# Softmax attention of a fused transformer block: score tiles of one PSUM bank in a written TensorE order, and sign projections as two products in fp32r

## The chip, the cores and the metric

The kernel runs on one core of one Trainium2 chip. The metric is the device time of one execution in microseconds. The kernel before takes 1735.04 us, the median of three runs (1726.19 to 1746.35). All profile numbers of the kernel before come from one profiled execution that took 1739.77 us.

## The reference, cut to what matters

Two batches of 1024 tokens with 512 features go through half a feed-forward layer, an attention layer and half a feed-forward layer again. The attention layer has 32 query heads of 16 features and 8 key and value heads, each of which serves four query heads. Its four projections use only the signs of their weights, with one scale for each output.

```python
def bitnet_linear(x, weight, scale_param):
    s = jnp.maximum(jnp.mean(jnp.abs(weight), axis=1), 1e-08)
    binary_w = jnp.sign(weight / s[:, None])
    y = jnp.einsum('bsi,oi->bso', x, binary_w)
    y = y * (s * scale_param)[None, None, :]
    return jnp.nan_to_num(y, nan=0.0, posinf=1000000.0, neginf=-1000000.0)
...
scores = jnp.einsum('bhqd,bhkd->bhqk', q, k) / np.sqrt(HEAD_DIM)
attn = jax.nn.softmax(scores, axis=-1)
out = jnp.einsum('bhqk,bhkd->bhqd', attn, v)
...
x = x + 0.5 * ffn(layernorm(x)); x = x + attention(layernorm(x)); x = x + 0.5 * ffn(layernorm(x))
```

Softmax is taken over all 1024 keys, without a mask, and the largest score of each query is subtracted ahead of the exponential.

## The kernel before, in words

Everything is in 32-bit floats. [...]operands of type F32R are multiplied in one pass with fewer mantissa bits, so a value that must be kept to full precision is split into a high part and the rest, and both are multiplied.

For each batch the kernel runs these stages: `ffn` (L152) on two groups of 512 tokens; `qkv` (L241) on the same groups; `attention` (L283); then for each group `o_proj` (L392), `ffn` and the store. For the first batch `binarize` (L218) turns the four projection weights, which the POOL queue loads at the start, into signs after the first `ffn`.

`qkv` makes the normalized input transposed (`ln_T`, L130), multiplies it with the sign weights in F32 (L255, L274), scales it on ScalarE (L258), replaces values that are not numbers (`nan_to_num`, L115: three or four VectorE instructions and one on GpSimd), and splits it into the high part and the rest on GpSimd (L261, L262). For queries 16 small DMAs on SP's queue for each chunk of 128 features (L268) put the parts in `qn`: each head has 32 rows, 16 of the high part and 16 of the rest, and four heads that share a key head fill the 128 rows.

`attention` works on one key head (four query heads) at a time. `place` (L287) copies the key's two parts to the four row groups with 16 DMAs on SP's queue (L293). `maxima` (L297) multiplies queries by keys (L308) and takes the largest score of each query on VectorE, 1024 scores in an instruction (L311). After 512 queries the maxima are transposed (L318), split on VectorE (L320, L321) and put by 8 DMAs on SP's queue (L327) in the tile `mq`. `scores` (L330) multiplies keys by queries again, now with keys on the rows of the output (L340), adds the negative maxima as one more product with a matrix of ones (L344), and takes the exponential on ScalarE, 1024 scores in an instruction (L347). `values` (L353) multiplies the exponentials by the values and by a column of ones, so the sums come out beside the outputs (L357, in F32); after 1024 keys the result is transposed (L364) and divided by the sums (L367, L368).

The loop at L376 runs `scores` of one key head and `maxima` of the next one in 16 alternating steps; each step also has the `values` of the step before. A score tile `p` covers two PSUM banks, and a pool of three such tiles (`psb`) is shared by `maxima`, `scores` and parts of `ffn`. Other products use a pool of two single banks (`pss`). `kT` and `mq` have two buffers.

The order of instructions on each engine is made when the program is built: a scheduler takes, for each engine, the instruction that it reckons to be ready first, earlier ones of the program ahead of later ones, and a tile can't be taken before its buffer is free. On the chip each engine works through its own list in that order, and so does SP's queue of DMAs.

Of the kernel before, what the change touches and what calls it, by code (L numbers as in the profile page):

```python
# [32 lines left out]
def macaron_kernel(ctx: ExitStack, tc: tile.TileContext, x_in, wbT, b_base, wrT, aT, bT,  # L33
# [11 lines left out]
    p3 = ctx.enter_context(tc.tile_pool(name="p3", bufs=3))  # L45
    tmp = ctx.enter_context(tc.tile_pool(name="tmp", bufs=7))
    sm = ctx.enter_context(tc.tile_pool(name="sm", bufs=4))
    ps_b = ctx.enter_context(tc.tile_pool(name="ps_b", bufs=3, space=bass.MemoryType.PSUM))
    ps_s = ctx.enter_context(tc.tile_pool(name="ps_s", bufs=2, space=bass.MemoryType.PSUM))

    def t512(name):
        return tmp.tile([P, 512], F32, tag="t512", name=name)

    def psb(name):
        return ps_b.tile([P, 2, 512], F32, tag="psb", name=name)

    def pss(name):
        return ps_s.tile([P, 512], F32, tag="pss", name=name)
# [21 lines left out]

    wq = const.tile([P, KC, D], F32, name="wq")
    wk = const.tile([P, KC, P], F32, name="wk")
    wv = const.tile([P, KC, P], F32, name="wv")
    wo = const.tile([P, KC, D], F32, name="wo")
    for t, src in ((wq, wqT), (wk, wkT), (wv, wvT), (wo, woT)):
        nc.gpsimd.dma_start(t, src.rearrange("(c p) n -> p c n", p=P))
# [20 lines left out]

    ones_r = const.tile([P, P], F32R, name="ones_r")
    nc.gpsimd.memset(ones_r.bitcast(F32), 1.0)
    vaug = big1.tile([P, NT, G, 32], F32, tag="vaug", name="vaug")  # L110
    nc.gpsimd.memset(vaug, 0.0)
    nc.gpsimd.memset(vaug[:, :, :, HD:HD + 1], 1.0)


    def nan_to_num(y, o, shape, n):  # L115
# [8 lines left out]
        nc.vector.tensor_scalar(lo_, y, 0.0, None, ALU.min)  # L124
# [5 lines left out]
    def ln_T(xt, n):  # L130
# [10 lines left out]
        xT = p2.tile([P, KC, GT], F32, tag="xT", name=f"xT{n}")  # L141
        for t in range(TG):
            xn = t512(f"xn{n}_{t}")
            nc.vector.tensor_scalar(xn, xt[:, t, :], mv[:, t, 0:1], rstd[:, t:t + 1],  # L144
                                    ALU.subtract, ALU.mult)
            pt = pss(f"pt{n}_{t}").rearrange("p (c q) -> p c q", c=KC)
            for c in range(KC):
                nc.tensor.transpose(pt[:, c, :], xn[:, c * P:(c + 1) * P], ident)  # L148
            nc.scalar.copy(xT[:, :, t * P:(t + 1) * P], pt)  # L149
        return xT  # L150

    def ffn(xt, n):  # L152

        xT = ln_T(xt, n)
        ph = psb(f"ph{n}").rearrange("p a (b n) -> p (a b) n", b=2)
        for t in range(TG):
            for c in range(KC):
                nc.tensor.matmul(ph[:, t, 0:ER + E], xT[:, c, t * P:(t + 1) * P], arw[:, c, :],  # L158
                                 start=(c == 0), stop=(c == KC - 1))
        lg = ph[:, :, ER:ER + E]  # L160
# [33 lines left out]
        for t in range(TG):  # L194
            nc.vector.tensor_tensor(
                hw[:, t * ER:(t + 1) * ER].rearrange("p (e r) -> p e r", e=E),
                ph[:, t, 0:ER].rearrange("p (e r) -> p e r", e=E),
                w01[0][:, t, :].unsqueeze(2).to_broadcast([P, E, R]), ALU.mult)
        pt = pss(f"hwp{n}")
# [4 lines left out]
        for t2 in range(TG // 2):  # L204
            pb = psb(f"pb{n}_{t2}")
            for j in range(2):
                t = 2 * t2 + j
                xb = t512(f"xb{n}_{t}")
                nc.gpsimd.tensor_tensor(xb, xt[:, t, :], bh, ALU.add)
                for c in range(KC):  # L210
                    nc.tensor.matmul(pb[:, j, :], xT[:, c, t * P:(t + 1) * P], wb[:, c, :],  # L211
                                     start=(c == 0), stop=False)
                nc.tensor.matmul(pb[:, j, :], hT[:, t * P:(t + 1) * P], lb, start=False, stop=True)  # L213
                nc.vector.scalar_tensor_tensor(xt[:, t, :], pb[:, j, :], 0.5, xb,  # L214
                                               ALU.mult, ALU.add)


    def binarize(w, n_out, name):  # L218
        ab = p2.tile([P, KC, GT], F32, tag="xT", name=f"ab_{name}")
        nc.scalar.activation(ab[:, :, 0:n_out], w, AF.Abs)  # L220
        pm = pss(f"pm_{name}")
        for c in range(KC):
            nc.tensor.matmul(pm[:, 0:n_out], ones, ab[:, c, 0:n_out],
                             start=(c == 0), stop=(c == KC - 1))
        s = tmp.tile([P, 512], F32, tag="t512", name=f"s_{name}")[:, 0:n_out]
# [5 lines left out]
        nc.scalar.activation(w, w, AF.Sign)  # L231
        return s

    def to_column(s, c, sc):

        pt = pss(f"col_{sc.name}_{c}")
# [4 lines left out]
    def qkv(b):  # L241

        qn = big1.tile([P, G, S], F32R, tag="qn", name=f"qn{b}")
        kn = [big1.tile([P, S], F32R, tag=f"kn{j}", name=f"kn{j}_{b}") for j in range(2)]
        for g in range(NG):
            n = f"a{b}_{g}"
            xT = ln_T(xg[b, g], n)
            cols = slice(g * GT, (g + 1) * GT)
            for c in range(KC + 1):
                w_, sc_ = (wq[:, :, c * P:(c + 1) * P], qsc[:, c:c + 1]) if c < KC else (wk, ksc)  # L250
                dst = ([p2.tile([P, 512], F32R, tag=f"qh{j}", name=f"qh{j}{n}_{c}") for j in range(2)]
                       if c < KC else [t[:, cols] for t in kn])
                pq = pss(f"pq{n}_{c}")
                for k in range(KC):
                    nc.tensor.matmul(pq, w_[:, k, :], xT[:, k, :],  # L255
                                     start=(k == 0), stop=(k == KC - 1))
                y = t512(f"y{n}_{c}")
                nc.scalar.activation(y, pq, AF.Copy, scale=sc_)  # L258
                z = t512(f"z{n}_{c}")
                nan_to_num(y[:, :], z[:, :], [P, 512], f"{n}_{c}")  # L260
                nc.gpsimd.tensor_copy(dst[0], z)  # L261
                nc.gpsimd.tensor_tensor(dst[1], z, dst[0].bitcast(F32), ALU.subtract)  # L262
                if c < KC:

                    for h in range(2 * REP):
                        for j in range(2):
                            r = 32 * (h % REP) + HD * j
                            nc.sync.dma_start(  # L268
                                qn[r:r + HD, 2 * c + h // REP, cols].bitcast(F32),
                                dst[j][h * HD:(h + 1) * HD, :].bitcast(F32))  # L270
            pv = pss(f"pv{n}").rearrange("p (t v) -> p t v", t=TG)
            for t in range(TG):
                for k in range(KC):
                    nc.tensor.matmul(pv[:, t, :], xT[:, k, t * P:(t + 1) * P], wv[:, k, :],  # L274
                                     start=(k == 0), stop=(k == KC - 1))
            y = t512(f"yv{n}").rearrange("p (t v) -> p t v", t=TG)
# [196 lines left out]
```

## Time and profile before

| | |
|---|---|
| time of the profiled execution | 1739.77 us |
| its span | 1738.0 us |
| median of three runs | 1735.04 us |
| busy: TensorE, VectorE, ScalarE, GpSimd | 1370.9, 950.0, 583.5, 147.5 us |
| TensorE clock granted, mean | 0.877 |
| 0 to 98 us | `ffn` of the first batch, `binarize` |
| 98 to 207.8 us; 950 to 1060 us | `qkv` and the first `place`, batch 0 and 1 |
| 207.8 to 789 us; 1060 to 1624 us | `attention`, batch 0 and 1 |
| 789 to 899 us; 1624 to 1738 us | `o_proj`, `ffn`, store, batch 0 and 1 |
| 899 to 950 us | `ffn` of batch 1 |

A row of the profile's groups names line, engine, operation, output and inputs, shapes and count; then come the busy time, the mean duration of one in ns, and the idle time of the engine ahead of it with what ended it. PE is TensorE, PEld its weight loads, DVE VectorE, ACT ScalarE, POOL GpSimd and SPq the queue of SP. In a timeline a row has the start, the length in us, the instruction and how many were merged, and in brackets the idle time ahead.

### The profile page before, as it was taken

What the parts mean: (1) busy time and instruction counts of PE and PEld (TensorE: products, weight loads), DVE (VectorE), ACT (ScalarE), POOL (GpSimd) and SP (SyncE); (2) the same over time, 40 slices, a digit from 0 to 9 for tenths busy, and PEclk for the clock granted to TensorE, in tenths of its full rate; (3) what the DMA queues carried; (4) which work ended last, traced back from release to release, by engine and by line L of the source; (5) the groups of instructions that cost most, each with busy time, mean ns of one, the idle gap of its engine ahead of it and who ended that gap; (6) DMA issues with size and microseconds to landing.
All of it is one profiled execution on the core that took longest, in us unless ns stands there. A gap on an engine that the chain in (4) does not pass through costs nothing.

```text
span 1738.0 us, 21741 instructions
## 1 busy us (share of the span) xinstructions
PE 1370.9 (79%) x8741; PEld 633.6 (36%) x8741; DVE 950.0 (55%) x1322; ACT 583.5 (34%) x653; POOL 147.5 (8%) x146
## 2 busy tenths in 40 slices
PE   5784398888888888897799806888888888888796
PEld 3442143333333333334354403433333333333353
DVE  3753276566665655624544616756665666663443
ACT  1210014354443434472011100344453444446310
POOL 3433000000000000002021420000000000000111
PEclk9897559799997979998999855799997989999898
DMA  4012400100101101000110223010110101100000
GB/s 159 0 27 47 72 2 1 25 16 11 25 2 25 21 6 26 1 2 0 49 49 1 45 49 53 2 26 1 25 17 11 26 1 26 22 5 2 1 25 24
DMA packets 31587, 40.31 MB, mean 23 GB/s; under 512 B 17264, under 2 KB 17776, under 8 KB 31488
## 3 DMA queue, kind: packets, MB, share of 16 engines
q1 hardware_dynamic: 28800, 34.13, 9.8%
q0 software_dynamic: 960, 3.21, 0.5%
q10 hardware_dynamic: 1728, 1.59, 0.3%
q8 instruction: 69, 1.13, 0.3%
q14 instruction: 30, 0.25, 0.0%
HBM read 9.00 MB, written 4.19 MB: 8 GB/s over the span
## 4 chain that ended last, share of the span: by engine, by line
PE 63%; ACT 13%; DVE 10%; SPq 7%; issue 3%; POOL 2%; DMA 2%; ACTq 0%; POOLq 0%; DVEq 0%
PE av L357 16%; PE p L308 14%; ACT es L347 12%; PE p L340 10%; SPq L268 6%; PE p L344 5%; DVE mn L311 3%; PE pbs L211 2%; PE pbf L211 2%; PE po L404 2%; PE pqa L255 2%; PE avT L364 1%; SPq L293 1%; PE mp L318 1%; PE phs L158 1%
## 5 line engine op out<-in xcount | busy, mean ns | idle before, releaser
L311 DVE TENSOR_REDUCE mn<-p 128x2 f32<-128x1024 f32 x512 | 617.9, 1221 | 402.1 <-PE p L308 399.1
L347 ACT ACTIVATE es<-p 128x1024 f32<-128x1024 f32 x512 | 499.2, 1022 | 730.1 <-PE p L344 714.4
L308 PE MATMUL p<-kT,qn 32*128 32x512 f32 x2048 | 400.4, 483 | 234.5 <-ACT es L347 125.6
L308 PEld LDWEIGHTS p<-kT,qn 32*128 32x128 f32 x2048 | 195.4, 213 | 404.0 <-ACT es L347 211.0
L357 PE MATMUL av<-es,vaug 128*32 128x512 f32 x2048 | 316.0, 656 | 0.1
L340 PE MATMUL p<-qn,kT 32*128 32x512 f32 x2048 | 269.8, 479 | 14.1 <-DVE mn L311 14.1
L340 PEld LDWEIGHTS p<-qn,kT 32*128 32x128 f32 x2048 | 115.3, 201 | 246.2 <-ACT es L347 140.0
L344 PE MATMUL p<-mq,ones_r 2*128 2x512 f32 x1024 | 163.8, 427 | 0.0
L127 POOL TENSOR_SCALAR ro<-yo 128x512 f32<-128x512 f32 x16 | 11.6, 723 | 1326.1 <-DVE yo L125 1303.7
L344 PEld LDWEIGHTS p<-mq,ones_r 2*128 2x128 f32 x1024 | 79.8, 203 | 20.6 <-issue 9.0
L357 PEld LDWEIGHTS av<-es,vaug 128*32 128x32 f32 x2048 | 43.4, 111 | 105.3 <-issue 100.4
L367 DVE RECIPROCAL rc<-avT 128x16 f32<-128x16 f32 x32 | 8.2, 258 | 125.1 <-PE avT L364 125.1
L255 PE MATMUL pqa<-xTa,wq 128*128 128x512 f32 x128 | 60.0, 629 | 2.8 <-ACT xTa L149 2.8
L211 PE MATMUL pbs<-wb,xTs 128*128 128x512 f32 x128 | 59.8, 597 | 0.9 <-DVE x L214 0.9
L211 PE MATMUL pbf<-wb,xTf 128*128 128x512 f32 x128 | 58.8, 594 | 0.0
L404 PE MATMUL po<-wo,aT 128*128 128x512 f32 x128 | 56.0, 595 | 0.5 <-ACT aT L400 0.5
L148 PE MATMUL pts<-ident,xns 128*128 128x128 f32 x64 | 14.8, 420 | 41.5 <-DVE xns L144 41.5
L149 ACT COPY xTs<-pts 128x512 f32<-128x512 f32 x16 | 9.3, 586 | 103.1 <-PE pts L148 103.1
L214 DVE SCALAR_TENSOR_TENSOR x<-pbs,xbs 128x512 f32<-128x512 f32 x16 | 11.1, 691 | 51.3 <-PE pbs L213 51.3
L320 DVE CAST mT<-mp 4x512 fp32r<-4x512 f32 x32 | 21.7, 679 | 31.4 <-PE mp L318 24.5
L364 PE MATMUL avT<-ident,avs 128*128 128x128 f32 x128 | 24.1, 297 | 18.3 <-ACT avs L361 17.4
L255 PEld LDWEIGHTS pqa<-xTa,wq 128*128 128x128 f32 x128 | 25.5, 202 | 35.3 <-issue 31.2
(172 smaller groups left out, 903.9 us busy)
## 6 DMA issues: line engine op xcount, KB each, us to landing
kT<-kn SPq DMA_DIRECT2D x256, 64.0 KB, 2.5
x<-in_x SPq DMA_DIRECT2D x4, 1024.0 KB, 6.2
qn<-qh0a SPq DMA_DIRECT2D x128, 32.0 KB, 2.0
qn<-qh1a SPq DMA_DIRECT2D x128, 32.0 KB, 1.9
mq<-mT SPq DMA_DIRECT2D x256, 2.0 KB, 1.7
out<-x SPq DMA_DIRECT2D x4, 1024.0 KB, 4.3
wb<-in_wbT ACTq DMA_DIRECT2D x1, 1024.0 KB, 20.4
wq<-in_wqT POOLq DMA_DIRECT2D x1, 1024.0 KB, 10.5
```

The costliest lines, as they stand in the source:

```text
L211: nc.tensor.matmul(pb[:, j, :], xT[:, c, t * P:(t + 1) * P], wb[:, c, :], start=(c == 0), stop=False)
L255: nc.tensor.matmul(pq, w_[:, k, :], xT[:, k, :], start=(k == 0), stop=(k == KC - 1))
L268: nc.sync.dma_start(qn[r:r + HD, 2 * c + h // REP, cols].bitcast(F32), dst[j][h * HD:(h + 1) * HD, :].bitcast(F32))
L308: nc.tensor.matmul(ps[:, j, :], qT[r0:r0 + 32, qt * P:(qt + 1) * P], kT[r0:r0 + 32, i, kh * 512:(kh + 1) * 512], start=(i == 1), stop=(i = ...
L311: nc.vector.tensor_reduce(mn[:, kh, qt % 4, 2 * hp:2 * hp + 2], ps, AX.X, ALU.max, negate=True)
L320: nc.vector.tensor_copy(mT[:, 0, :], pt[0:REP, :])
L340: nc.tensor.matmul(ps[:, j, :], kT[r0:r0 + 32, i, keys], qT[r0:r0 + 32, cols], start=(i == 1), stop=False)
L344: nc.tensor.matmul(ps[:, j, :], ones_r[r0:r0 + 2, :], mq[r0:r0 + 2, cols], start=False, stop=True)
L347: nc.scalar.activation(e, ps, AF.Exp, scale=HD ** -0.5)
L357: nc.tensor.matmul(av[0][32 * h:32 * h + 32, :], vaug[:, kt, g, :], es[h // 2][:, h % 2, :], start=(kt == 0), stop=(kt == NT - 1))
L364: nc.tensor.transpose(pt[:, t * P:(t + 1) * P], avs[:, t * P:(t + 1) * P], ident)
L404: nc.tensor.matmul(po, aT_[:, c, t * P:(t + 1) * P], wo[:, c, :], start=(c == 0), stop=(c == KC - 1))
```

## The change

Scores. A score tile is one bank of 512 columns for one head; seven banks form one pool `w` for all products, and one bank is kept for the outputs. A unit is now 512 queries of one key head, 16 in a batch, and takes four turns. A turn has eight tiles of maxima, `m`, in two passes each, eight tiles of exponentials, `e`, in three passes each (the third adds the maxima), and four parts `A` of the output product, each of 256 columns for four heads. The string `TURN` writes down the TensorE order of a turn; `manual_schedule` keeps TensorE to it, while the other engines are ordered by the scheduler as before. A unit's exponentials start five turns after its maxima, its outputs one turn later.

Queries and keys. `qkv` runs for one group and writes both parts of queries and keys to DRAM, two DMAs for each chunk. `place` reads them back with 8 DMAs for queries and 8 for keys for each unit, all on SP's queue; `q` and `k` have three buffers, `mq` two.

Sums. The output tile with its sums goes to DRAM in one DMA for each unit. `normalized` reads outputs and sums back (16 DMAs for each of four chunks in each group of queries), takes the reciprocals, writes them to DRAM (1 DMA) and reads them back spread over the rows (8 DMAs); GpSimd multiplies and splits, ScalarE makes the high part.

Projections. The sign weights are F32R, and inputs are a high part and the rest, so each F32 product becomes two F32R products (`qkv`, `o_proj`). `binarize` loads its weight when its turn comes. In `nan_to_num` the minimum goes from VectorE to GpSimd; the split's high part goes from GpSimd to ScalarE; in `o_proj` the last addition goes to GpSimd. In `ffn` the router's logits are copied out by ScalarE. All of `vaug` starts as ones.

```diff
-    tmp = ctx.enter_context(tc.tile_pool(name="tmp", bufs=7))
+    tmp = ctx.enter_context(tc.tile_pool(name="tmp", bufs=8))
-    ps_b = ctx.enter_context(tc.tile_pool(name="ps_b", bufs=3, space=bass.MemoryType.PSUM))
-    ps_s = ctx.enter_context(tc.tile_pool(name="ps_s", bufs=2, space=bass.MemoryType.PSUM))
+    ps = ctx.enter_context(tc.tile_pool(name="ps", bufs=7, space=bass.MemoryType.PSUM))
+    ps_a = ctx.enter_context(tc.tile_pool(name="ps_a", bufs=1, space=bass.MemoryType.PSUM))
...
-        nc.vector.tensor_scalar(lo_, y, 0.0, None, ALU.min)
+        nc.gpsimd.tensor_scalar(lo_, y, 0.0, None, ALU.min)
...
+            if halves:
+                nc.vector.tensor_tensor(xL[:, :, tok], pt, xT[:, :, tok].bitcast(F32), ALU.subtract)
...
+            nc.scalar.copy(lg[:, 2 * t2:2 * t2 + 2, :], ph[:, :, ER:ER + E])
...
+    def binarize(src, n_out, name):
+        w = p2.tile([P, KC, GT], F32, tag="xT", name=f"w_{name}")[:, :, 0:n_out]
+        nc.gpsimd.dma_start(w, src.rearrange("(c p) n -> p c n", p=P))
+        ab = p2.tile([P, KC, GT], F32, tag="xL", name=f"ab_{name}")[:, :, 0:n_out]
...
+        wr = const.tile([P, KC, n_out], F32R, name=f"sign_{name}")
+        nc.scalar.activation(wr, w, AF.Sign)
...
+    def qkv(b, g):
+        xs = ln_T(xg[b, g], n, True)
...
+            pq = bank(f"pq{n}_{c}")
+            for k in range(KC):
+                for j in range(2):
+                    nc.tensor.matmul(pq, w_[:, k, :], xs[j][:, k, :],
+                                     start=(k + j == 0), stop=(k + j == KC))
...
+            hi = t512(f"hi{n}_{c}", F32R)
+            nc.scalar.copy(hi, z)
+            lo = t512(f"lw{n}_{c}", F32R)
+            nc.gpsimd.tensor_tensor(lo, z, hi.bitcast(F32), ALU.subtract)
+            for j, t in enumerate((hi, lo)):
+                dst = qd[b][j, c * P:(c + 1) * P, cols] if c < KC else kd[b][j, :, cols]
+                nc.sync.dma_start(dst, t.bitcast(F32))
...
+    TURN = ("m0(0) e0(2) e0(7) e0(5) m1(0) e1(2) e1(5) e1(7) m0(4) e2(2) e2(7) m0(1) m1(4) m0(7) "
+            "m1(1) A0 A1 m1(7) e2(5) m0(6) e0(4) e0(3) e0(1) m1(6) e1(4) e1(3) e1(1) m0(2) e2(4) "
+            "e2(3) e2(1) m1(2) A2 m0(3) e0(0) e0(6) m0(5) m1(3) e1(0) e1(6) m1(5) e2(0) e2(6) A3")
+    TU = NT // 2
+    LEAD = TU + 1
...
+        def place(u):
...
+            q = p2.tile([P, 512], F32R, tag="q", name=f"q{n}", bufs=3)
+            for h in range(REP):
+                for j in range(2):
+                    r = 32 * h + HD * j
+                    f = (REP * g + h) * HD
+                    nc.sync.dma_start(q[r:r + HD, :].bitcast(F32), qd[b][j, f:f + HD, cols])
+            k = p2.tile([P, 2, S], F32R, tag="k", name=f"k{n}", bufs=3)
+            src = kd[b][:, g * HD:(g + 1) * HD, :].rearrange("i d s -> d i s")
+            for r in range(0, P, HD):
+                nc.sync.dma_start(k[r:r + HD, :, :].bitcast(F32), src)
...
+        def m_tile(u, i, p):
...
+            nc.tensor.matmul(s["m", i], s["q"][rows, qt * P:(qt + 1) * P],
+                             s["k"][rows, 1 - p, kh * 512:(kh + 1) * 512],
+                             start=(p == 0), stop=(p == 1))
+            if p == 1:
+                nc.vector.tensor_reduce(s["mn"][:, h, qt, kh:kh + 1], s.pop(("m", i)), AX.X,
+                                        ALU.max, negate=True)
...
+        def m_place(u):
+            pt = bank(f"mp{b}_{u}")
+            nc.tensor.transpose(pt[0:4 * REP, 0:P], s["mm"], ident)
+            mT = sm.tile([4 * REP, 2, P], F32R, tag="mT", name=f"mT{b}_{u}")
+            nc.vector.tensor_copy(mT[:, 0, :], pt[0:4 * REP, 0:P])
+            nc.vector.tensor_tensor(mT[:, 1, :], pt[0:4 * REP, 0:P], mT[:, 0, :].bitcast(F32),
+                                    ALU.subtract)
+            for h in range(REP):
+                for j in range(2):
+                    r = 32 * h + j
+                    nc.sync.dma_start(
+                        s["mq"][r:r + 1, :].bitcast(F32),
+                        mT[h * 4:(h + 1) * 4, j, :].bitcast(F32))
...
+        def e_tile(u, i, p):
...
+            if p < 2:
+                nc.tensor.matmul(t, s["k"][rows, 1 - p, kt * P:(kt + 1) * P], s["q"][rows, :],
+                                 start=(p == 0), stop=False)
+            else:
+                two = slice(32 * h, 32 * h + 2)
+                nc.tensor.matmul(t, ones_r[two, :], s["mq"][two, :], start=False, stop=True)
+                e = p2.tile([P, 512], F32, tag="es", name=f"es{b}_{u}_{i}", bufs=20)
+                nc.scalar.activation(e, s.pop(("e", i)), AF.Exp, scale=HD ** -0.5)
...
+        def a_part(u, kt, half):
...
+            if kt == NT - 1 and half == 1:
+                o = t512(f"avs{b}_{u}")
+                nc.scalar.copy(o, s["av"])
+                nc.sync.dma_start(ad[b][g, :, qb * 512:(qb + 1) * 512], o)
...
+        with tc.manual_schedule(engines={mybir.EngineType.PE}):
+            place(0)
+            for n in range(TU * len(units) + LEAD + 1):
+                m, e, a = todo(n, 0), todo(n, LEAD), todo(n, LEAD + 1)
+                if m and m[1] == 0 and m[0] + 1 < len(units):
+                    place(m[0] + 1)
+                for kind, p, i in turn:
...
+                        if p == 0 and n >= TU and (n % TU) == 0 and (n // TU - 1) < len(units):
+                            m_place(n // TU - 1)
...
+    def normalized(b, qb):
...
+        for c in range(KC):
+            rs = sm.tile([P, 32], F32, tag="rs", name=f"rs{n}")
+            z = t512(f"an{n}")
+            for g2 in range(2):
+                for h in range(REP):
+                    r = (g2 * REP + h) * HD
+                    nc.sync.dma_start(rs[r:r + HD, :], ad[b][2 * c + g2, 32 * h + HD, cols].rearrange(
+                        "(s x) -> s x", x=32))
+                    nc.sync.dma_start(z[r:r + HD, :], ad[b][2 * c + g2, 32 * h:32 * h + HD, cols])
+            nc.vector.reciprocal(rs, rs)
+            nc.sync.dma_start(rd[b][qb, c * 8:(c + 1) * 8, :].rearrange("h (s x) -> (h s) x", x=32), rs)
+            rb = t512(f"rb{n}")
+            for h in range(8):
+                nc.sync.dma_start(rb[h * HD:(h + 1) * HD, :],
+                                  rd[b][qb, c * 8 + h, :].partition_broadcast(HD))
+            nc.gpsimd.tensor_tensor(z, z, rb, ALU.mult)
+            nc.scalar.copy(hs[0][:, c, :], z)
+            nc.gpsimd.tensor_tensor(hs[1][:, c, :], z, hs[0][:, c, :].bitcast(F32), ALU.subtract)
```

The diff is cut: `m_gather`, which joins the two halves of a unit's maxima on VectorE, and `todo`, which gives unit and turn from the number of the turn, are told above.

## The prediction

> **What bounds the kernel now.** I read the chain that ended last first, then busy time by stage, then the timeline of one step, then SP's queue and the waits.
>
> The chain says that TensorE sets the end for 63% of the span, with ScalarE's exponentials and VectorE's maxima behind it. The groups give the price of each:
>
> ```profile
> PE 63%; ACT 13%; DVE 10%; SPq 7%; issue 3%; POOL 2%; DMA 2%; ACTq 0%; POOLq 0%; DVEq 0%
> ...
> L311 DVE TENSOR_REDUCE mn<-p 128x2 f32<-128x1024 f32 x512 | 617.9, 1221 | 402.1 <-PE p L308 399.1
> L347 ACT ACTIVATE es<-p 128x1024 f32<-128x1024 f32 x512 | 499.2, 1022 | 730.1 <-PE p L344 714.4
> L308 PE MATMUL p<-kT,qn 32*128 32x512 f32 x2048 | 400.4, 483 | 234.5 <-ACT es L347 125.6
> ```
>
> All four engines wait for one another: maxima for TensorE, TensorE for ScalarE to empty a tile. By stage (stretch, length, busy PE, PEld, DVE, ACT, POOL, then granted clock):
>
> ```profile
> 207.80:251.00 43.20, 41.76 (x166) 20.34 (x170) 38.56 (x38) 4.10 (x4) 0.00 (x0) 0.50 0.11 17
> ...
> 318.00:789.00 471.00, 402.60 (x3098) 170.59 (x3091) 260.53 (x255) 223.74 (x236) 0.00 (x0) 0.91 0.08 13
> ...
> 789.00:899.00 110.00, 86.89 (x300) 48.10 (x299) 56.39 (x157) 12.04 (x23) 20.43 (x21) 0.89 0.05 20
> 98.00:207.80 109.80, 51.68 (x175) 27.43 (x175) 42.08 (x60) 9.71 (x16) 32.47 (x33) 0.73 0.25 51
> ```
>
> Attention takes 581 + 564 = 1145 of 1738 us. In `qkv` (last row) no engine is busy even half of the time: 106 us of the chain are SP's issues at L268. One step of attention, in order of time:
>
> ```profile
> 561.31 0.75 PE L340 MATMUL p<-qn,kT 32*128 32x512 f32 x8
> 561.88 0.41 PE L344 MATMUL p<-mq,ones_r 2*128 2x512 f32 x4
> 562.11 0.64 PE L308 MATMUL p<-kT,qn 32*128 32x512 f32 x4
> 563.45 0.74 PE L308 MATMUL p<-kT,qn 32*128 32x512 f32 x4 [0.70 <-ACT es L347]
> 564.12 1.07 PE L357 MATMUL av<-es,vaug 128*32 128x512 f32 x8
> 565.11 0.76 PE L340 MATMUL p<-qn,kT 32*128 32x512 f32 x8
> ```
>
> The step lasts 565.11 − 561.31 = 3.80 us. Four matmuls on four row groups, a wave, follow one another every 562.11 − 561.88 = 0.23 us. The first wave after a change to another tile shape takes 0.34 (561.31 to 561.88 is two waves). The second L308 group waits 0.70 us for a tile and fills two row groups only. The output product takes 565.11 − 564.12 = 0.99 us. SP's queue around a key head's start:
>
> ```profile
> 309.17 10.90 SPq L293 DMA_DIRECT2D kT<-kn  x16
> 320.17 41.60 SPq L327 DMA_DIRECT2D mq<-mT  x16
> 383.82 10.99 SPq L293 DMA_DIRECT2D kT<-kn  x16
> 394.91 36.26 SPq L327 DMA_DIRECT2D mq<-mT  x16
> ```
>
> In the individual issues one follows another every 0.632 us whatever its size, and the `kT` DMAs stand ahead of the `mq` ones.
>
> **What the skill says.** The Trainium skill, "TensorEngine Tiling (Array Packing)", Key Properties: a change of tiling mode drains TensorE. The trace agrees: 0.34 instead of 0.23 us for the first wave, and about 0.1 ahead of each output block. "TensorE: Matmul & The Clock Gate", Measured speedup vs the span model: four 32-row matmuls of 512 columns gain 3.07 times; four in 0.23 us is about that or better here. "FP8 and Floating Point Precision", TensorE Precision Notes: a true FP32 product is four passes. The trace agrees: one tile of four products at L255 takes 3.43 us (start to start), 0.86 each or four times 0.215, so two one-pass products halve it. "DMA: Bandwidth & Descriptors", Issuing engines are not separate DMA queues, calls issue time usually small beside the transfer; here it is 0.63 us against 1.7 to 2.5 us to landing, and a queue of 16 is no longer small.
>
> **The change part by part.**
>
> *A full turn of attention* (two old steps). TensorE: reading TURN in groups without a repeated row group gives 11 waves for 40 matmuls: 11 × 0.23 = 2.53. Outputs: A0 with A1 is one old block, 0.99; A2 and A3 alone are half the stream (0.43) with the same entry (0.13) and a bit for twice the weight loads: 0.6 each; 2.19 together. Three changes of shape add 0.11 behind and 0.10 ahead: 0.63. Sum 5.35 us. VectorE: eight maxima of 512; rows of that size take 0.683 us alone and 0.60 start to start (799.46, 800.07, 800.67 in the timeline): 4.8, and 0.2 for a quarter of gather and split: 5.0. ScalarE: a copy of 512 takes 0.587, 0.49 start to start: 8 × 0.49 + 0.15 = 4.1. So TensorE stays the bound, with VectorE close. Bounds: 5.35 if every bank is free in time, 6.5 if maxima don't overlap (8 × 0.69 plus handshakes). I take 5.7, which leaves 0.35 for waits on the seven banks.
>
> *Turns in a batch*: 70. 59 full: 336. Five with maxima only, VectorE-bound at 4.9: 24.5. Five with exponentials and outputs: 9 waves and the blocks, 5.0 each, 25. One with outputs: 2.5. Sum 388.
>
> *The maxima's way to `mq`.* In a unit's fifth turn the transposes stand at A0, 1.25 us after its start (four waves, 1.03, and a change of shape); transposes and split on VectorE (0.3 each, behind one maximum) end near 2.65. Then 8 issues × 0.632 = 5.1 and 1.7 to landing: row group 3 lands at 9.4. TensorE wants it at e2(7), in the third wave of the next turn: 5.7 + 0.9 (change of shape 0.1, two waves 0.57, issue 0.2) = 6.6. In order behind it stand all later matmuls, so VectorE and ScalarE run dry too. 2.8 us a unit, 16 units: 45 a batch. Bounds: 0 (earlier landing) and 15.1 a unit (rival B). Attention: 388 + 45 = 433 a batch against 581 and 564: −279 in both.
>
> *SP inside attention*: 16 + 8 + 1 issues a unit are 15.8 us of 25.6. `place` itself has three turns for 10.1 + 2.5 us and is hidden; without that cover it costs up to 12.6 a unit. The DMAs of `normalized` for the first 512 queries are ready while the second half runs, and their buffers come free with the output tiles, so I expect them there: 100 issues, 63 us over eight units. That fills SP to 93%, and I charge 15 us a batch for bursts ahead of `mq`: +30. Bounds 0 and 60 a batch.
>
> *`qkv`*: SP's 64 issues a group (40 us) become 10. TensorE goes from 3.43 to 1.7 us a chunk. GpSimd is now the slowest: 0.75 + 0.77 + 1.41 = 2.9 us a chunk (the clamp's row twice, L262 once). Five chunks at about 3.5, since five temporaries a chunk share eight buffers, and 3.5 for values make 21 a group; both groups 42, 8 for the last chunk's chain and its write, 12 for the first reads (16 × 0.63 + 2.5). 62 a batch instead of 110: −96. The four extra subtractions on VectorE (0.69 each) are hidden by GpSimd. The values' product has 128 columns in one pass, which no row shows: between a quarter and all of today's 3.7 us a group; hidden either way.
>
> *`o_proj`*: products go from 14 to 7 us a group, and VectorE's chain loses two instructions, but GpSimd's gets an addition of 1.29. The first group waits for the last spread sums: last output DMA 2, 8 issues 5, landing 2, GpSimd 3, about 12 against 4 now. The second group's tiles are free only as the first `ffn` ends: 64 issues, 40 us, of which I expect 12 to show. Net +5 a batch: +10. If nothing is issued early it is +60 a batch.
>
> *`binarize`*: the output weight's load waits for a buffer and then takes about 6 us (the input's time): +8, bounds 0 and 15. The logits' copies on ScalarE, 0.2 each, and the new `vaug` fill: nothing, beside 51 us for two `ffn` that TensorE fills.
>
> *Sum*, against the profiled execution: 1738 − 279 + 30 − 96 + 10 + 8 = 1411 of span, 1413 with the 1.8 us around it. Its 1739.77 stands 4.7 above the median of 1735.04, so 1408.
>
> **The rivals.** *A: no waits.* The turn runs at 5.35, `mq` comes in time and SP's bursts cost nothing: 1408 − 118 × 0.35 − 90 − 30 = 1247. For it: in the stretch with exponentials and outputs alone, TensorE already packs four row groups at clock 1.0. Against it: 0.632 us an issue.
>
> *B: `place` goes ahead of `mq` on SP (the other side).* Place: the fifth turn of each unit, where `place` of the unit after next waits for the last e1 of an older unit, some 4.5 us into the turn. If it stands ahead of the eight `mq` DMAs, those land at 4.5 + 10.1 + 5.1 + 1.8 = 21.5 and TensorE stands 15 us, 12.3 more than I count: 32 × 12.3 = 394, 1802. For it: today `kT` goes ahead of `mq` at every key head. Against: today `kT` is free first (383.82, and `mT` is split later), in the new order `mT` is ready first (2.65 against 4.5). It decides from 11 us more a unit, which needs all 16 ahead of all eight.
>
> *C: the same queue, mixed*, with some `place` or `normalized` DMAs between the eight: 3 to 9 us more a unit, 1500 to 1690, say 1590.
>
> *D: the change does not pack.* If single-bank tiles still wait in rotation, a turn stays at 6.5 or more: 1408 + 118 × 0.8 = 1502; I count it with C.
>
> **How the numbers follow.** My forecast 0.50 (own range 1310 to 1490), A 0.22, C with D 0.18, B 0.10. I predict 1408. Below 1230 I leave 0.06, above 1630 0.13, so the range is 1230 to 1630. About 1% is what a measurement of this kernel can tell from no change: 1718 to 1752. Faster: all of the forecast and A, nearly all of C: 0.89. Within 1%: C's end, 0.02. Slower: B, 0.09.
>
> **What would show it.** A turn of 5.5 to 5.9 us in the timeline; TensorE waiting 2 to 3 us for `mq` once in four turns (15 would be B); SP's issue order with `mq` ahead of `place`; `qkv` near 62 us a batch with GpSimd busiest; 100 early issues of `normalized` inside attention. I am wrong if TensorE waits for VectorE on most tiles, if attention is over 480 us a batch, or if the tail after attention grows by more than 30.

## The result, and the profile after

The changed kernel takes 2082.01 us (median of four runs, 2068.40 to 2094.94); the kernel before took 1740.69 beside it (four runs, 1726.19 to 1749.34). The ratio is 1.197, 95% interval 1.1843 to 1.2097: slower by a fifth, where 1408 was forecast. The profiled execution took 2068.4 us, its span is 2066.6, and the mean granted clock fell from 0.877 to 0.720. In ratios and their intervals the runs of a kernel that took over 1.5% longer than its fastest are left out; medians are of all runs.

The chain that ended last, and the costliest groups of the kernel after (name, count, then busy time, mean ns of one, idle time before and what ended it):

```profile
PE 45%; SPq 18%; DMA 12%; DVE 11%; issue 6%; POOL 6%; ACT 2%; DVEq 0%; POOLq 0%; ACTq 0%
...
L318 DVE TENSOR_REDUCE mn<-m 128x1 f32<-128x512 f32 x1024 | 653.4, 684 | 558.8 <-PE m L314 464.6
L314 PE MATMUL m<-k,q 32*128 32x512 f32 x2048 | 534.2, 524 | 59.5 <-DMA k<-kd 59.5
L356 PE MATMUL e<-mq,ones_r 2*128 2x512 f32 x1024 | 331.6, 497 | 351.5 <-DMA k<-kd 197.7
```

TensorE's share of the chain went from 63% to 45%, while SP's queue and the DMAs went from 9% to 30%. VectorE's maxima cost what was forecast (684 ns). The new thing is in the last row: the product that adds the maxima waits 351.5 us in all. In the kernel before its counterpart waited for nothing; the product that stood there, 234.5 us in all, was that of the maxima (L308).

```profile
L344 PE MATMUL p<-mq,ones_r 2*128 2x512 f32 x1024 | 163.8, 427 | 0.0
```

By stage of the kernel after (stretch, length, busy PE, PEld, DVE, ACT, POOL, then granted clock, DMA share, GB/s):

```profile
127.00:214.00 87.00, 34.41 (x165) 27.71 (x165) 32.21 (x54) 15.18 (x26) 41.53 (x35) 0.68 0.31 84
214.00:845.00 631.00, 446.88 (x4369) 216.44 (x4369) 337.25 (x565) 265.39 (x494) 0.00 (x0) 0.73 0.22 38
...
885.00:1067.00 182.00, 87.42 (x254) 52.54 (x247) 57.09 (x139) 12.44 (x25) 62.55 (x51) 0.65 0.13 36
```

Against the forecast's 1411 of span the excess is 655.6: attention 671 and 658 us instead of 433 and 15 of bursts each (433 too long in all); the tails 182 and 191 instead of 115 and 119 (139); `qkv` 87 and 90 instead of 62 (53); the start 127 instead of 106 (21); the middle `ffn` 60 instead of 51 (9).

Part of one unit of attention on TensorE. The first two rows begin output blocks A0, the last two are products that wait (in brackets: the idle time ahead of each):

```profile
386.76 1.07 PE L368 MATMUL av<-es,vaug 128*32 128x256 f32 x16
...
392.83 1.07 PE L368 MATMUL av<-es,vaug 128*32 128x256 f32 x16
...
398.90 0.46 PE L356 MATMUL e<-mq,ones_r 2*128 2x512 f32 x1 [0.77 <-DMA mq<-mT]
411.48 0.76 PE L356 MATMUL e<-mq,ones_r 2*128 2x512 f32 x1 [12.11 <-DMA k<-kd]
```

A turn from A0 to A0 takes 6.07 us with the transpose in it, near the 5.7 of the forecast. But once a unit TensorE stands: 0.77 us for the maxima of one head's row group, and 12.11 for those of the next. SP's queue around it tells why:

```profile
393.98 4.37 SPq L339 DMA_DIRECT2D mq<-mT  x7
398.45 3.62 SPq L298 DMA_DIRECT2D q<-qd  x8
402.11 3.68 SPq L302 DMA_DIRECT2D k<-kd  x8
405.84 0.58 SPq L339 DMA_DIRECT2D mq<-mT  x1
```

Seven of the eight transfers of the maxima go first, as the forecast reckoned. The eighth stands behind the 16 of `place`, and TensorE's fixed order needs all eight. The profile names `k` as the releaser, but this product reads only `mq` and `ones_r`, so the eighth `mq` is what is late. It is issued at 405.84, while the keys fill the DMA engines (their busy share is 1.00 from 404 to 410), and TensorE goes on only 5.6 us later. What the clock does at such a wait, in stretches of 6 us of the same run (the sixth number of a row, after the busy times, is the clock):

```profile
362.00:368.00 6.00, 0.00 (x0) 0.00 (x0) 0.00 (x0) 0.00 (x0) 0.00 (x0) 0.50 0.93 116
...
374.00:380.00 6.00, 6.00 (x48) 2.50 (x49) 3.07 (x5) 3.62 (x7) 0.00 (x0) 0.50 0.09 33
380.00:386.00 6.00, 6.00 (x65) 2.74 (x65) 4.42 (x7) 3.85 (x8) 0.00 (x0) 0.76 0.05 13
386.00:392.00 6.00, 6.00 (x82) 3.17 (x79) 5.45 (x11) 4.31 (x9) 0.00 (x0) 1.00 0.01 3
```

TensorE works again from 369.26, and has half its clock until about 383. In 374 to 380 it gets 48 products done, in 386 to 392, at full clock, 82.

### The profile page after: what moved, and what is told of

The parts are those of the page before. It is cut to its first block, busy times and chain, and to the rows that moved or that the text cites. A ratio compares the mean times of both kernels' runs of the same rounds, so it can differ in the third digit from the quotient of the medians.

```text
span 2066.6 us, 26722 instructions
## 1 busy us (share of the span) xinstructions
PE 1334.4 (65%) x10501; PEld 696.8 (34%) x10501; DVE 933.0 (45%) x1746; ACT 649.4 (31%) x1201; POOL 253.6 (12%) x213
## 4 chain that ended last, share of the span: by engine, by line
PE 45%; SPq 18%; DMA 12%; DVE 11%; issue 6%; POOL 6%; ACT 2%; DVEq 0%; POOLq 0%; ACTq 0%
PE av L368 14%; PE m L314 10%; DMA k<-kd 5%; PE e L352 5%; DVE mn L318 4%; SPq L339 4%; SPq L298 4%; SPq L302 4%; PE e L356 4%; DMA mq<-mT 3%; PE pbf L208 3%; PE pbs L208 3%; SPq L419 2%; SPq L414 2%; POOL loo L113 1%
## 5 line engine op out<-in xcount | busy, mean ns | idle before, releaser
L318 DVE TENSOR_REDUCE mn<-m 128x1 f32<-128x512 f32 x1024 | 653.4, 684 | 558.8 <-PE m L314 464.6
L358 ACT ACTIVATE es<-e 128x512 f32<-128x512 f32 x1024 | 550.9, 598 | 782.4 <-PE e L356 439.4
L314 PE MATMUL m<-k,q 32*128 32x512 f32 x2048 | 534.2, 524 | 59.5 <-DMA k<-kd 59.5
L356 PE MATMUL e<-mq,ones_r 2*128 2x512 f32 x1024 | 331.6, 497 | 351.5 <-DMA k<-kd 197.7
L352 PE MATMUL e<-q,k 32*128 32x512 f32 x2048 | 394.0, 505 | 6.6 <-DVE mn L318 5.7
L368 PE MATMUL av<-es,vaug 128*32 128x256 f32 x4096 | 375.3, 472 | 0.0
L314 PEld LDWEIGHTS m<-k,q 32*128 32x128 f32 x2048 | 274.5, 228 | 276.6 <-issue 155.9
L356 PEld LDWEIGHTS e<-mq,ones_r 2*128 2x128 f32 x1024 | 158.4, 226 | 386.9 <-DMA k<-kd 305.3
L352 PEld LDWEIGHTS e<-q,k 32*128 32x128 f32 x2048 | 184.5, 221 | 37.5 <-DVE mn L318 15.2
L368 PEld LDWEIGHTS av<-es,vaug 128*32 128x32 f32 x4096 | 107.6, 124 | 205.3 <-issue 184.4
L139 PE MATMUL pts<-ident,xns 128*128 128x128 f32 x64 | 17.1, 432 | 94.3 <-DVE xns L135 94.3
L114 DVE SCALAR_TENSOR_TENSOR ya<-ya,loa 128x512 f32<-128x512 f32 x20 | 13.9, 693 | 76.8 <-POOL loa L113 76.8
L139 PEld LDWEIGHTS pts<-ident,xns 128*128 128x128 f32 x64 | 11.9, 220 | 100.7 <-DVE xns L135 100.7
```

The costliest lines, as they stand in the source:

```text
L314: nc.tensor.matmul(s["m", i], s["q"][rows, qt * P:(qt + 1) * P], s["k"][rows, 1 - p, kh * 512:(kh + 1) * 512], start=(p == 0), stop=(p == 1))
L318: nc.vector.tensor_reduce(s["mn"][:, h, qt, kh:kh + 1], s.pop(("m", i)), AX.X, ALU.max, negate=True)
L352: nc.tensor.matmul(t, s["k"][rows, 1 - p, kt * P:(kt + 1) * P], s["q"][rows, :], start=(p == 0), stop=False)
L356: nc.tensor.matmul(t, ones_r[two, :], s["mq"][two, :], start=False, stop=True)
L358: nc.scalar.activation(e, s.pop(("e", i)), AF.Exp, scale=HD ** -0.5)
L368: nc.tensor.matmul(s["av"][32 * h:32 * h + 32, cols], vaug[:, kt, g, :], s["es"][kt * REP + h][:, cols], start=(kt + half == 0), stop=(kt ...
```

## The experiments

Times are of one run each unless runs are named. Beside place_after, mq_pool_queue, half_the_keys and fill_the_wait the kernel before was run once, at 1766.3 us; beside the later kernels its medians of 7 to 11 runs were 1742 to 1745. Its single runs lie between 1722 and 1766, so some 25 us between two single runs mean little.

| kernel | us | clock |
|---|---|---|
| changed kernel | 2068.4 (the profiled run) | 0.720 |
| fill_the_wait | 2059.26 | 0.856 |
| half_the_keys | 1949.07 | 0.737 |
| buffers_and_min_only | 1962.16 | 0.720 |
| place_after | 1741.93 | 0.757 |
| mq_pool_queue | 1726.81 | 0.764 |
| turn_later | 1635.86 | 0.797 |
| two_queues | 1573.58 | 0.824 |
| two_queues_own | 1508.49 | 0.825 |
| all_parts | 1512.71 (six runs, 1495.43 to 1519.48) | 0.832 |
| two_queues_own_min, twice | 1473.62 (four runs); 1448.34 (six, 1423.71 to 1469.70) | 0.829; 0.842 |

The theory ahead of the first runs: the order on SP holds the attention up, and the clock multiplies it. The rivals: the keys' transfers themselves (1 MB for each unit) are too slow; or the time goes elsewhere in the turn.

**place_after.** `place` is called after the turn's products instead of ahead of them:

```diff
-                if m and m[1] == 0 and m[0] + 1 < len(units):
-                    place(m[0] + 1)
                 for kind, p, i in turn:
...
                     m_gather(m[0])
+                if m and m[1] == 0 and m[0] + 1 < len(units):
+                    place(m[0] + 1)
```

> Theory O (order on SP): the last of a unit's eight mq DMAs stands behind the 16 DMAs of place, and TensorE waits some 13 us for it in 28 of 32 units, after which its clock stays at half for about 15 us more. With place written after the turn's instructions all eight mq DMAs go first: the 12 to 13 us wait falls below 3 us, a unit from 42 to about 28 us (what the last units, which have no place, take), and the time to 1660 to 1730 us. Theory T (transfers): the megabyte of keys fills the DMA engines and holds mq wherever it stands; then a unit stays at 38 us or more and the time above 1950 us.

Measured: 1741.93, 326 us less. SP's queue now has `mq` eight times, then `q`, then `k`. So the order of one transfer on one queue cost 326 of 2068 us. The same megabytes now move behind it, and the products that add the maxima no longer wait for them. A unit falls from 42.5 to 29.1 us (means of 12 and 13 units, from transpose to transpose). It is still not the 23.0 that four turns take where nothing waits (units of 22.8 to 23.0 occur in several of these kernels), and the clock stays at 0.757. In its timeline TensorE's products wait, once a unit:

```profile
300.64 0.47 PE L356 MATMUL e<-mq,ones_r 2*128 2x512 f32 x1 [0.77 <-DMA mq<-mT]
301.87 0.76 PE L356 MATMUL e<-mq,ones_r 2*128 2x512 f32 x1 [0.77 <-DMA mq<-mT]
```

and stretches of the same run show what follows:

```profile
293.00:299.00 6.00, 5.85 (x77) 2.91 (x77) 5.72 (x12) 4.27 (x9) 0.00 (x0) 1.00 0.02 4
...
305.00:311.00 6.00, 6.00 (x45) 2.80 (x49) 3.27 (x5) 3.57 (x7) 0.00 (x0) 0.50 1.00 160
```

Two waits of 0.77 us, and the next 10 us run at half clock. In the two batches 23 of 28 such pairs were followed by 3.4 to 13.7 us of it, and five by none. Four of those five units took 25.0 to 25.1 us instead of 29, with the same waits. So of the 6 us over a clean unit about 2 are the waiting and 4 the clock. (No unit of place_after was without waits: the one of 25.0 that the expectation of two_queues calls so is one of these.)

Which pairs count can be read on the clock's own steps: every change of the clock in these traces lies on a grid of 3.41 us. Two pairs, in stretches of that grid:

```profile
297.97:301.39 3.42, 2.37 (x24) 0.82 (x18) 1.98 (x4) 1.61 (x4) 0.00 (x0) 1.00 0.01 4
301.39:304.80 3.41, 2.93 (x21) 1.12 (x21) 1.29 (x2) 0.94 (x2) 0.00 (x0) 0.50 0.23 67
...
356.00:359.41 3.41, 2.64 (x28) 1.32 (x26) 2.50 (x4) 1.88 (x4) 0.00 (x0) 1.00 0.04 8
359.41:362.83 3.42, 2.65 (x34) 1.42 (x36) 1.50 (x3) 1.32 (x3) 0.00 (x0) 1.00 0.20 56
```

The first pair leaves TensorE busy for 69% of one stretch, and the next stretch has half the clock. The second pair is split over two stretches with 77% each, and the clock stays.

**mq_pool_queue.** `place` stays where it is; the eight `mq` transfers are issued by GpSimd (`nc.gpsimd.dma_start` at L339).

> The eight mq DMAs are issued from GpSimd's queue, which has nothing else to do in attention; SP's list is otherwise as it was. Theory O: the wait goes as when place comes later, 1650 to 1750 us. Theory T: mq shares the DMA engines with the keys' megabyte and still waits 5 us or more at each unit: 1800 us or more.

Measured: 1726.81. The same wait is gone by another way, so it was the place in SP's queue and not anything else that moving `place` does. Here too some 1.1 to 1.6 us of waiting for `mq` are left in most units (eight issues of 0.51 us), and the clock is 0.764.

**half_the_keys.** Order as in the changed kernel, but only the high part of the keys is moved (`[P, 1, S]`), and used twice.

> Left out: the low part of the keys; place moves half a megabyte of keys instead of one, with as many DMAs, and the high part is used in both passes. Theory T gives part of the wait to the transfers: it gets shorter by about 3.5 us, and the time by about 100 us, to 1930 to 1990 us. If only the number of issues counts, the time stays within 2040 to 2090 us.

Measured: 1949.07, inside the range. The last `mq` is issued at 379.21 and TensorE goes on at 381.11, 1.9 us later instead of 5.6. So the 12 us wait is some 8 us of SP's 16 issues and some 4 us in which the keys fill the DMA engines. Both stand in front of the eighth `mq`, and place_after takes away both.

**fill_the_wait.** Sixty products into a bank that nothing reads stand ahead of e2(2) in a unit's first exponential turn, to keep TensorE working through the wait:

```diff
+                    if (kind, p, i) == ("e", 2, 2) and e and e[1] == 0:
+                        d = bank(f"d{b}_{n}")
+                        for x in range(60):
+                            nc.tensor.matmul(d, wq[:, 0, 0:P], wq[:, 0, :], start=(x == 0), stop=(x == 59))
```

> Sixty products of 128 x 512 of no use, about 13 us of TensorE at full clock, stand ahead of the third pass that waits for mq in each unit; SP's order is as it was. Theory C (the clock): the wait itself does not go, but TensorE stays busy in it and keeps its full clock, so the unit gets shorter by the 5 to 8 us that the half clock costs after the wait: 1830 to 1930 us although work was added. If the clock plays no part, the time is 2060 us or more.

Measured: 2059.26; the size expected did not come. The clock rose to 0.856 and the wait for `mq` is gone (0.6 us in all), and a good unit takes 36.9 us: 13.9 of sixty products and 23.0 of turns. But every second unit takes 40 to 45: VectorE's maxima come late after the sixty products, TensorE waits 1.35 us for one (at 423.85), and the granted clock is 0.50 in 427 to 433. The fill also costs more than the wait it covers. This run shows the price of a clean unit, and does not by itself separate wait and clock.

Two more kernels, each different from place_after in one thing, take only the last 1.5 us away and so separate them.

**two_queues.** place_after, with the low halves of the maxima issued by GpSimd beside SP:

```diff
-                    nc.sync.dma_start(
+                    (nc.sync, nc.gpsimd)[j].dma_start(
                         s["mq"][r:r + 1, :].bitcast(F32),
```

> `place` is issued after the turn, as in place_after, and the eight transfers of the maxima are issued by two queues: the high halves by SP, the low halves by GpSimd, which has nothing else to do in the attention; the issue of the eight takes some 2.5 us instead of 5. In place_after a unit took 29.4 us with two waits of 0.77 us for `mq` and about 10 us at half clock after them; a unit without any wait took 25.0 there, and four turns at full clock take 22.9. Theory (a short wait costs mostly by the clock that is granted after it): 24 to 26 us a unit, 1560 to 1630 us, clock over 0.83. Rival (the clock falls for another reason, only the idle itself goes): 1.5 us a unit, 1680 to 1710 us, clock still near 0.76.

Measured: 1573.58. The waits of TensorE for `mq`, in place_after and then in two_queues (total, times, longest):

```profile
PE e L356 <- DMA mq<-mT: 48.9, 64, 2.3
```

```profile
PE e L356 <- DMA mq<-mT: 13.5, 16, 1.5
```

35 us of waiting less gave 168 us of time. The rest is clock (0.824, against 0.757): units of 22.8 to 24.0 us stand where 29 to 31 stood, with some at 26 to 32 left. The rival (idle time alone) had 1680 to 1710 and falls. The Trainium skill, "DMA: Bandwidth & Descriptors", Issuing engines are not separate DMA queues, says that a second issuing engine saves only the sequencer's time; the runs agree, 2.45 us of issue instead of 4.97, and here this was what TensorE waited for.

**turn_later.** place_after with `LEAD = TU + 2`: one queue, but the exponentials a turn later.

> place_after (one queue for the maxima) with a unit's exponentials started six turns after its maxima instead of five; the deal of the work is otherwise the same. The last maxima landed about 2 us late in place_after and now have 5.7 us more. Theory (the wait and the clock after it were the whole difference between a unit of 29.4 and one of 23): no wait for `mq`, 23 to 24 us a unit, one turn more a batch (some 5 us each): 1560 to 1620 us, as two_queues or a little above. Rival (the second queue itself, by relieving SP, made two_queues fast): 1680 us or more.

Measured: 1635.86, above the range. The part about the units holds: no wait for `mq`, and 24.5 us a unit in the first batch against 24.0 in two_queues (13 units each), so it is the lateness and not the second queue. What was missed is the end of each batch, exponentials and outputs alone. First turn_later, then two_queues:

```profile
601.00:660.00 59.00, 58.03 (x368) 24.50 (x368) 2.61 (x7) 26.76 (x50) 0.00 (x0) 0.51 0.02 7
```

```profile
601.00:630.00 29.00, 27.52 (x310) 12.56 (x305) 0.70 (x3) 22.15 (x42) 2.05 (x4) 1.00 0.04 13
```

After a wait of 2.1 us that ended at 601.7 turn_later was at half clock, and there it stayed for 58 us though TensorE was busy 98% of the time. From the last transpose to the last output product the two ends take 29 us longer each than in two_queues, the one more turn included. That is nearly all of the loss of 62.

**two_queues_own.** Buffers of their own for `an` and `rb` in `normalized`:

```diff
-            z = t512(f"an{n}")
+            z = p2.tile([P, 512], F32, tag="nz", name=f"an{n}", bufs=3)
...
-            rb = t512(f"rb{n}")
+            rb = p2.tile([P, 512], F32, tag="nr", name=f"rb{n}", bufs=3)
```

> As two_queues, with buffers of their own for the gathered outputs and the reciprocals' rows (three each, instead of the shared twelve 128x512 ones). Theory (the tail's 64 issues stayed behind the attention because they waited for buffers): those of each batch go out while the second half of the attention runs, the stretch after the attention falls from about 190 to 130 to 150 us, so 80 to 120 us less than two_queues. Rival (SP then issues them in front of the maxima, and the clock falls again): less than 40 us gained, or a loss.

Measured: 1508.49, 65 us less, between the two expectations. From the last output product to the end takes 128 us instead of 192, and the first batch's tail is as much shorter. But the output products span 419 and 407 us instead of 379 and 385. The rival's reason for that is not shown: the early transfers do stand between the maxima on SP, yet TensorE waits 14.3 us in all for `mq`, against 13.5. Of the 40 and 22 us, 20 and 17 lie behind the last transpose, where exponentials and outputs alone run at half clock here (0.50 and 0.57) and ran at full clock in two_queues. Why the clock fell there was not tried.

**two_queues_own_min.** In addition the minimum of L113 is back on VectorE.

> As two_queues_own, and the minimum of the nan replacement is back on VectorE (the row of before: 0.42 us; on GpSimd it takes 1.49 and 1.73 us in the changed kernel). Theory (it is in the chunk's serial chain, and slows the next operation of VectorE beside it from 0.69 to 1.48 us): 1.5 to 2 us for each of some 20 chunks and 16 output tiles on the path, 50 to 70 us less than two_queues_own; 1370 to 1450 us in all, as the prediction had it. Rival (VectorE or the transfers bind there): within 20 us of two_queues_own.

Measured: 1473.62, where 50 to 70 us less than 1508.49 was expected, then 1448.34 in the repeat: 35 to 60 us less. All ten runs lie below the one of two_queues_own. The profiles show where: TensorE's three longest waits outside the units, for the transposes' inputs (L139, `pts` and `pta`) and for the keys at the start of attention (L314), fall from 182.9 to 144.7 us. The size stays uncertain, since two_queues_own has one run.

> The kernel of two_queues_own_min in five rounds against the kernel before, for its interval. It took 1416 to 1481 us there. 1440 to 1480 us, 0.83 to 0.85 of before.

The ratio to before is 0.8244, interval 0.8175 to 0.8312: this version is faster than the kernel before and the changed kernel.

**all_parts.** The same with `LEAD = TU + 2`.

> two_queues_own_min with the exponentials six turns after the maxima. Theory: the six or so units a batch that still took 27 to 31 us there (waits of 1.3 to 1.5 us, then half clock) fall to 23.5, which is 5 us for each, less 5 us a batch for the longer start and end: 1400 to 1440 us, and less spread between runs than the 1416 to 1481 of two_queues_own_min. Rival (the remaining drops of the clock come from waits for VectorE's maxima, not from `mq`): within 20 us of 1474.

Measured: 1512.71, slower than without; the theory fell. The drops of the clock that are left don't come from `mq`. TensorE's eight idle times over 0.9 us in the first batch, after the start, stand ahead of L314 and L331, maxima and their transpose: five wait for VectorE, three for the keys' transfers. The extra turn is some 6 us a batch; why the rest was lost is open. The ratio is 0.8688 (0.8642 to 0.8734).

**buffers_and_min_only.** Own buffers and minimum, with `place` left ahead.

> The changed kernel with the own buffers for the gathered outputs and the minimum on VectorE, and with `place` left ahead of the last maximum. In two_queues_own and two_queues_own_min these two were worth 65 and 35 us. Theory (they lie outside the attention and the order of SP's queue is a separate cost): 1960 to 1990 us. Rival (the early transfers of `normalized` come in front of the maxima on SP too, where a fifth of them counts once the whole queue is late): over 2000 us.

Measured: 1962.16, as the theory had it, and 106 us less than the profiled run of the changed kernel, against 100 to 125 in the other order of steps. So these two are separate from the order on SP.

## Why the prediction was wrong

**The step that failed** is "The maxima's way to `mq`". Its arithmetic stood: the transposes, 0.62 us an issue, and in place_after, where all eight go first, a wait of 1.5 us a unit where 2.8 was charged. What failed is the sentence that kept rival B small: "It decides from 11 us more a unit, which needs all 16 ahead of all eight." One transfer of eight behind the 16 is enough, since the fixed order of TensorE needs the last one. The prediction priced the wait about rightly (15.1 us as its upper bound, measured 12.1 and 0.8), and asked the wrong question about it: whether `mT` is ready ahead of `place`, which it is, instead of whether the last of eight issues can be overtaken. Why the scheduler put `place` in front of the eighth was not tried. place_after puts the price at 326 us.

**A term that was missing**: the clock after a wait. The sum took a wait at its own length. A changed unit of 42.5 us is 23.0 of four clean turns, 12.9 of waiting (12.11 + 0.77), and 6.6 more. The half clock explains most of that: TensorE works at it for some 13 us after the wait (369.26 to 383), and a turn there takes 9.5 us (A0 at 370.42 to A0 at 379.90) instead of 5.75. In place_after, of 29.1, it is 1.5 of waiting and 4.6 more, and the units there with these waits and no half clock took 25.0. The "What would show it" part named a wait of 2 to 3 us once in four turns as the forecast's own sign. Even 1.5 us of it cost 6.1 a unit: place_after had the forecast's order and took 1742. With the waits nearly gone, two_queues' first attention (214 to 629) takes 415 us, against the 448 forecast for it. The Trainium skill, "TensorE: Matmul & The Clock Gate", What's actually happening, gives the half clock after an idle window of about 3.4 us and the full one after about as long a busy one, with windows that run freely. The traces agree on half and full and on the window (the grid of 3.41 us). They differ in what a window needs: 31% of one idle was enough at 297.97 in place_after, and then one to four windows at half clock follow in its units, though TensorE is busy.

**The turn** was right, in mechanism too: 5.7 forecast, and 23.0 us for four are 5.75 each. In a clean unit of two_queues (361.62 to 384.60, 22.98 us) TensorE is busy 22.77 us and VectorE 21.09, so TensorE is the bound with VectorE close, as said. Rival D falls. Rival A falls too: even turns without a wait don't run at 5.35.

**The tail** failed in "`their buffers come free with the output tiles, so I expect them there: 100 issues`". Only the sums and reciprocals, 36 for a group, went early; `an` and `rb` share eight tiles (not twelve, as the expectation of two_queues_own has it) with all other 128x512 temporaries. SP after the end of attention, in the changed kernel:

```profile
886.47 3.21 SPq L414 DMA_DIRECT2D an<-ad  x7
889.73 3.66 SPq L419 DMA_DIRECT2D rb<-rd  x8
...
911.94 3.66 SPq L419 DMA_DIRECT2D rb<-rd  x8
```

That is 29 us of issues where 12 was charged, and the second group's come again after the first `ffn` (951 to 1005). The prediction's own bound, "if nothing is issued early it is +60 a batch", is close: the tails grew by 72 and 77. The value taken was +5. SP's bursts, charged at 15 us a batch for the early issue, did not show as waits when two_queues_own had it (14.3 us for `mq` in both batches, against 13.5).

**`qkv`**: the products in F32R did what was forecast, 0.23 us each at full clock (L248, start to start) where one in F32 took 0.86. The stage failed on "GpSimd is now the slowest: 0.75 + 0.77 + 1.41". The minimum was priced by the clamp's row. The changed kernel's groups:

```profile
L113 POOL TENSOR_SCALAR loa<-ya 128x512 f32<-128x512 f32 x20 | 29.7, 1487 | 20.0 <-ACT ya L251 20.0
L113 POOL TENSOR_SCALAR loo<-yo 128x512 f32<-128x512 f32 x16 | 27.7, 1733 | 16.0 <-DVE yo L437 16.0
...
L114 DVE SCALAR_TENSOR_TENSOR yo<-yo,loo 128x512 f32<-128x512 f32 x16 | 23.7, 1480 | 22.1 <-POOL loo L113 22.1
```

Twice the 0.75. And GpSimd takes the next chunk's minimum only behind the last step of the chunk before (137.87 in the trace), so the whole chain sets the pace: minimum 1.5, VectorE 0.7, clamp 0.8, VectorE 0.7, ScalarE 0.6, GpSimd 1.3, with the steps between them 5.9 us a chunk where 3.5 was taken. The last row, VectorE's step at 1.48 us instead of 0.69, I first put down to the minimum; with the minimum on VectorE it still takes 1.38, so the minimum is not the cause. In two_queues_own_min it runs beside GpSimd's addition L440 (662.27 within 661.80 to 663.15); whether that slows it was not tried. `binarize` was on the side named ("+8, bounds 0 and 15") and 21 came; which part of it is not settled.

**The range** of 1230 to 1630 left 0.13 above it, and B had 0.09 and its price of 1802. B's mechanism came at 2082 with the clock and the tails on top. The forecast's 1408 is near what two_queues_own_min does (1448), and that kernel's tails (115 and 118 us) are near the forecast's too, so the sum priced the work. But it takes four mends to get there. What the sum left out is how the last transfer of a set is ordered, who holds a buffer, and what the clock makes of a wait.

## What to carry to other kernels

Where one engine's order is written by hand, look up for each wait in it the last transfer that ends it, and what can get in front of that one on its queue: being first with seven of eight is being late. Don't price a wait of TensorE at its length alone: 1.5 us of it cost 6.1 on average in place_after. Look at the granted clock just after it, in stretches of the clock's own grid. Before charging a transfer as early, name the buffer that it fills and who holds that buffer.

## What the runs showed of the hardware that was not expected

- What decides on the half clock goes with the idle share of a 3.41 us stretch of the grid more than with the length of a wait. In the twelve traces of the changed kernel and its variants, 3 of 2717 full-clock stretches in which TensorE was busy 90% or more were followed by half clock, 41 of 200 with 70 to 90%, 118 of 154 with 50 to 70%, and 322 of 398 with less. The share is not the whole rule: the kernel before, with 70 to 90% in 218 full-clock stretches, kept the full clock behind 202. So no length of a wait is safe or harmful by itself: a single one of 1.35 us (turn_later, 433.66) left the clock as it was, and one of 1.33 us (two_queues_own_min, 501.57) brought 10 us of half clock.
- A stage with exponentials and outputs alone has run at full clock (29 us in two_queues) and at half for its whole length (58 us in turn_later), with TensorE busy 95 and 98% of the time. In the second batch of two_queues_own it came in at full clock and fell to half at 1341.3. What brings it back is open.
- SP issues a transfer that reads DRAM every 0.46 us (8 in 3.62 to 3.68), one that reads the on-chip memory every 0.62 (8 in 4.97); GpSimd one of the latter every 0.51 (8 in 4.10, mq_pool_queue).
- On GpSimd a minimum alone takes 1.49 and 1.73 us for 128x512 (L113), minimum and maximum in one instruction 0.83 and 0.67 (L116).
